# Layer 1 of a two-layer graph and expert network: the graph in blocks of 12, 8 and 6 row tiles, two early slot tables, and token lists dealt on GpSimd between gathers

## The chip, the cores and the metric

The kernel runs on one core of one Trainium2 chip, as one launch. The metric is device time in microseconds. A profile of one execution shows what each engine did: PE is TensorE (PEld its weight loads), DVE is VectorE, ACT is ScalarE, POOL is GpSimd, SP is SyncE, which here only issues transfers. L followed by a number is a line of the kernel before.

## The reference

The input is a matrix x of 3327 rows and 256 columns and an adjacency matrix of 3327 by 3327. Two layers follow each other, each a graph step and an expert step, both added to x.

```python
x = x + gnn0(layernorm(x), adj)          # mean over neighbours, then a linear map
x = x + ffn0(layernorm(x))               # 16 experts, top 2
h = layernorm(x)
Wh = h @ W
e = (Wh @ a[:256])[:, None] + (Wh @ a[256:])[None, :]
att = softmax(where(adj == 0, -1e9, e), axis=1)
x = x + leaky_relu(att @ Wh, 0.2)
f = layernorm(x)
p = softmax(relu(f @ router_w1 + b1) @ router_w2 + b2)      # 6 experts
w, i = top_k(p, 2); w = softmax(w)
out[e] = relu(relu(f @ w1[e] + c1[e]) @ w2[e] + c2[e]) @ w3[e] + c3[e]
x = x + sum of w * out[i]
```

The change concerns the last seven lines, layer 1.

## The kernel before

Rows stand in 26 tiles of 128, the last with 127 rows. Four tiles make a chunk, so there are seven chunks, the last of two tiles.

**The graph step** (`graph`) works through blocks of chunks. `GRAPH` for layer 1 is chunks 0 to 2, then 3 and 4, then 5, then 6: blocks of 12, 8, 4 and 2 tiles. For a block it walks through groups of source rows: `load_adj` brings a piece of the transposed adjacency matrix (L708, on SP), `mask_of` turns it into a 0/1 mask on DVE (L719), and PE multiplies the weighted rows y by it (L840) into PSUM. A mask holds at most 1536 columns, so a group is one source tile in the first two blocks, three in the block of four tiles and six in that of two. Three adj and three mask buffers are kept.

When a block's products are done, ACT and DVE copy the sums out (aT, L853 and L854), and a `finish` generator is made for each of its chunks. A generator's steps are: the final product with w1x and the update of x (L783), centring and normalising (L263 to L275), the store of the rows to the DRAM tensor hd (L794), transposes (L800), the router (L1268, `choose` L868) and `dispatch`. The steps of one block are called between the groups of the next block, two generators in turn (`in_turn`). Those of the last block run after the graph.

**dispatch** picks two experts per row on DVE, counts rows by expert with a small product (L356 to L360), and writes one entry per row and choice into the DRAM tensor list, by an indirect transfer from POOL (L387), two of them for each row tile: 52 in layer 1. An entry holds the place of the result, the row and the weight. The running counts are in seen1.

**The expert step** works in slots of 256 entries of one expert. There are 29 in the usual case, and more in a branch. `slot_table` turns the counts into a table: expert and place of each slot. The first table (`routed1`) is made after the first block's rows are counted and holds EARLY1 = 7 full slots; the second, the final one, is made after all rows are counted. A slot needs: `places`, which loads its 256 entries (who, L608, SP); `rows_in`, two indirect gathers from hd (xg, L616, POOL); `turned`, the transposes (L633); `layer1` twice (L1299); `out1` (L1311), with bias and weight on DVE (L1314, L1316); and `rows_out`, two indirect scatters to zd (L641, POOL). `slots1` runs these as a pipeline: in iteration s, out1 of slot s - 1, the second layer of s, the first layer of s + 1, the transposes of s + 2, the gathers of s + 3. There are three xg buffers. Expert weights of slots 0 to 6 come by one transfer each (v from w1d, 898 KB, L601). Those of later slots are copied on DVE (L1333) out of w_all, all six experts' weights, which are loaded after the graph (L1327), in memory that the graph's pools had.

In the program's text the slots stand after the graph:

```python
    graph("1", GRAPH, prepare1, 0.0, OP.not_equal, wx[1], update1, after1, 8, {(2, 0): routed1}, pools=pools1, ahead=ahead1, ready=list(REST))
    graph1.close()
    ...
    slots1(0, USUAL1)
```

A scheduler orders each engine's instructions, within `issue_after` marks. It keeps reads and writes of one DRAM tensor in order: a who load waits for the list writes that stand before it in the program, and a list write for the who loads before it. Layer 0 already deals the lists of its last blocks one by one: they are put into the list `due` and called from the loop of its slots.

Of the kernel before, what the change touches and what calls it, by code (L numbers as in the profile page):

```python
# [25 lines left out]
def kernel(  # L26
# [37 lines left out]
    GRAPH = [CHUNKS[:3]]  # L64
    while sum(map(len, GRAPH)) < len(CHUNKS):
        c = sum(map(len, GRAPH))
        GRAPH.append(CHUNKS[c : c + (2 if len(CHUNKS) - c > 2 else 1)])
# [15 lines left out]

    NE = sum(map(len, GRAPH[0]))
    assert NE <= NF
    EARLY1 = -(-(2 * NE * P - E1 * (S1 - 1)) // S1)

    USUAL1 = min(SLOTS1, int(2 * N / S1 + E1 / 2 + (E1 / 12) ** 0.5))
    LATE1 = USUAL1 - E1
    LOW = CHUNKS[: 4 * len(CHUNKS) // 7]  # L90
    assert EARLY1 < LATE1 and len(LOW) >= len(GRAPH[0])

# [3 lines left out]
    GRAPH0 = [CHUNKS[:3], CHUNKS[3:4], CHUNKS[4:]]  # L96
    NE0 = sum(map(len, CHUNKS[:4]))
    assert NE0 <= NF and len(GRAPH0[2]) <= 3
# [26 lines left out]
    hd_of = dram_disjoint_views(hd[:, :], 2)  # L125
# [176 lines left out]
    def dispatch(blk, logits, E, rows_of, seen, second_softmax):  # L302
# [15 lines left out]
        where = wheres[second_softmax]  # L318
        m, s, p = col("t_m"), col("t_s"), full("t_p")
# [63 lines left out]
        issued = []  # L383

        def listed(j, i):
            with in_turn_on_pool() if not second_softmax else nullcontext():
                ins = nc.gpsimd.indirect_dma_start(  # L387
                    out=rows_of[2 * (t0 + j) + i],
                    out_offset=bass.IndirectOffsetOnAxis(ap=idx[:, i, j : j + 1], axis=0),
                    in_=where[:, t0 + j, i, :], in_offset=None, bounds_check=E * NP - 1, oob_is_err=False,  # L390
                )
            if not second_softmax and blk in GRAPH0[2]:
                last["pool"] = ins
            if len(issued) > 1 and second_softmax and blk is GRAPH[1][-1]:
                tc.add_manual_dep(ins.ins, issued[-2], mybir.DependencyInfo(mybir.DependencyClass.Sync, mybir.DependencyReason.DATA))
            issued.append(ins.ins.name)

        for j in range(n):
            for i in range(2):
                if not second_softmax and blk in GRAPH0[2]:  # L400
                    due.append(lambda j=j, i=i: listed(j, i))
                else:
                    listed(j, i)
# [76 lines left out]
    def slot_table(E, seen, size, slot_p, first=None, taken=None, low=None, late=None, finals=False):  # L480
# [13 lines left out]
        def small(name, w=E, dtype=F32):  # L494
            return work.tile([P, w], dtype, name=name + ("e" if first else ""), bufs=1)
# [97 lines left out]
    def expert(table, s, E):  # L593

        with in_order():
            return (nc.sync.value_load(table[s : s + 1, 0:1], min_val=0, max_val=E - 1),
                    nc.sync.value_load(table[s : s + 1, 2:3], min_val=0, max_val=1))

    def load(tile_, source, which):
        e, new = which  # L600
        last["who"] = nc.sync.dma_start(tile_, source(bass.ds(e, 1)), cond=new, bounds_check="skip_entire_dma")  # L601

# [8 lines left out]
    def rows_in(who, of):  # L611

        n = who.shape[1]
        xg = io.tile([P, n, D], F32, name="xg", bufs=5 if n == 1 else 3)
        for h in range(n):
            last["pool"] = nc.gpsimd.indirect_dma_start(  # L616
                out=xg[:, h, :], out_offset=None, in_=of,
                in_offset=bass.IndirectOffsetOnAxis(ap=who[:, h, 1:2], axis=0),
            )
        return xg  # L620
# [17 lines left out]
    def rows_out(s, who, y):  # L638
        n = who.shape[1]
        for h in range(n):  # L640
            last["z"] = nc.gpsimd.indirect_dma_start(  # L641
                out=zviews[n * s + h], out_offset=bass.IndirectOffsetOnAxis(ap=who[:, h, 0:1], axis=0),
                in_=y[:, h, :], in_offset=None, bounds_check=2 * NP - 1, oob_is_err=False,
            )
            if s < LATE1:
                z_ready.append(last["z"].ins.name)
# [35 lines left out]
    def of_chunk(views, blk, ne):  # L682
        return views[0 if blk[-1] < ne else 1]
# [17 lines left out]
    def load_adj(adjs, block, g):  # L701

        c0, c1, cols, ce = columns(block)
        kr = rows(g[0])
        a = group_tile(adjs, I32, "adj", g, ce)
        src = adj_t[g[0] * P : g[0] * P + kr * len(g), c0:c1]
        if kr == P:
            last["adj"] = nc.sync.dma_start(a[:, :, :cols], src.rearrange("(t p) i -> p t i", p=P))  # L708
        else:
            for lo, hi in last_rows():  # L710
                nc.sync.dma_start(a[lo:hi, 0, :cols], src[lo:hi, :])
        return a
# [28 lines left out]

    def in_turn(those):

        now = []
        while those or now:
            while those and len(now) < 2:
                now.append(those.pop(0))
            for one in list(now):
                try:
                    next(one)  # L750
                    yield
                except StopIteration:
                    now.remove(one)
# [3 lines left out]
    def graph_pools(name, st):  # L757
        y = st.enter_context(tc.tile_pool(name=f"y{name}", bufs=1, side="right")).tile([P, NT, 2, D], F32R, name=f"y{name}")
        return y, *(st.enter_context(tc.tile_pool(name=f"{n}{name}", bufs=b, side="right"))
                    for n, b in (("adjs", AHEAD), ("big", AHEAD), ("tmp", 4)))  # L760
# [6 lines left out]
    def graph(name, blocks, prepare, value, op, wx, update, after, steps, routed, between=None, pools=None, ahead=(), ready=None, over={}, finish_with=None):  # L767
        adj_ahead, masks_ahead = ahead or ({}, {})
        with ExitStack() as st:
            y, adjs, big, tmp = pools or graph_pools(name, st)  # L770

            def finish(blk, aT):
# [4 lines left out]
                for i, t in enumerate(blk):  # L777
# [10 lines left out]
                    if i == 1 or i == n - 1:  # L788
                        centered(blk[i // 2 * 2 : i + 1], mv)
                        yield  # L790
                h = norm_centered(blk, mv)
                if name == "0":
                    store(blk)
                nc.scalar.dma_start(of_chunk(hd_of, blk, NE0 if name == "0" else NE)[t0 * P : (t0 + n) * P, :].rearrange("(t p) d -> p t d", p=P), h[:, :n, :])  # L794
# [489 lines left out]
    def routed1():  # L1284
        early["table"], early["had"] = slot_table(E1, seen1, S1, slot_p1, first=EARLY1)
        for s in range(EARLY1):
            who[s] = places(early["table"], s, E1, lists[1], S1)
# [4 lines left out]
    def layer1(s, i, src):  # L1292

        ps = bank(2 if s < EARLY1 or i == 0 else 1, [P, NC1, S1])
# [11 lines left out]
    def out1(s, who, h2):  # L1306
        ps = bank(1 if s < EARLY1 else 0, [P, 2, D])
# [9 lines left out]
        rows_out(s, who, y)  # L1317

    who = {}
    graph("1", GRAPH, prepare1, 0.0, OP.not_equal, wx[1], update1, after1, 8, {(2, 0): routed1}, pools=pools1, ahead=ahead1, ready=list(REST))  # L1320
    graph1.close()

    held = ctx.enter_context(tc.tile_pool(name="held", bufs=1, side="right"))
    w1_all = held.tile([P, E1, BB + 2 * 2], F32, name="w1_all")
    for e in range(E1):
        with in_order():
            last["who"] = nc.sync.dma_start(w1_all[:, e, :], w1d[e])  # L1327

    def weights_of(s):

        with tc.issue_after(last["dve"].ins) if "dve" in last else nullcontext():
            e = nc.vector.value_load(table1_of(s)[0][s - EARLY1 : s - EARLY1 + 1, 0:1], min_val=0, max_val=E1 - 1)
        last["copy"] = nc.vector.tensor_copy(w1s[s % 3], w1_all[:, bass.ds(e, 1), :].rearrange("p o w -> p (o w)"))  # L1333

    table1 = slot_table(E1, seen1, S1, slot_p1, taken=early["had"], low=seen_low, late=LATE1 - EARLY1, finals=True)

    def table1_of(s):
        return (early["table"], s) if s < EARLY1 else (table1, s - EARLY1)

    xg, xT, h1, h2, zs = {}, {}, {}, {}, {}  # L1340

    def slots1(first, end):
        for s in range(first - 3, end + 1):
            if first <= s - 1 < end:
                out1(s - 1, who[s - 1], h2.pop(s - 1))
            if first <= s + 2 < end:
                if s + 2 < EARLY1:
                    load(w1s[(s + 2) % 3], lambda e: w1d[e].rearrange("o p w -> p (o w)"), expert(*table1_of(s + 2), E1))
                else:
                    weights_of(s + 2)  # L1350
            known = EARLY1 if s < EARLY1 - 2 else end
            for i in range(max(who, default=-1) + 1, min(s + 5, known)):
                who[i] = places(*table1_of(i), E1, lists[1], S1)
            for i in range(max(xg, default=-1) + 1, min(s + 4, known)):
                xg[i] = rows_in(who[i], hd_of[0][: NE * P, :] if i < EARLY1 else hd[:, :])
# [4 lines left out]
            if first <= s + 2 < end:  # L1360
                xT[s + 2] = turned(xg[s + 2], 1 if s + 2 < EARLY1 else -1)
# [4 lines left out]
            if not first and s == LATE1 - 4:  # L1366
                or_any(table1, early["bad"])
            if not first and s == LATE1 - 2:
                with in_order():
                    early["low"] = nc.sync.value_load(table1_of(USUAL1)[0][USUAL1 - EARLY1 : USUAL1 - EARLY1 + 1, 4:5], min_val=0, max_val=1)  # L1370
# [5 lines left out]
            for i in SUMMED.get(s - LATE1, ()) if not first else ():  # L1376
                with tc.issue_after(last["copy"].ins), tc.issue_after(last["dve"].ins):
                    summed(LOW[i], zs[i])
                stored(nc.sync, LOW[i], zs.pop(i))

    LOADED, SUMMED = {1: (0, 1), 2: (2, 3)}, {2: (0,), 3: (1,), 4: (2, 3)}
    assert len(LOW) == 4 and max(SUMMED) < E1
    tail = ctx.enter_context(tc.tile_pool(name="tail", bufs=len(CHUNKS)))
    slots1(0, USUAL1)

    with more(*early["more"]):
        slots1(USUAL1, SLOTS1)
# [45 lines left out]
```

## Time and profile before

| | |
|---|---|
| runs, median of 3 | 1059.12 us (1056.38 to 1060.92) |
| profiled execution, its own time | 1021.54 us |
| its span, first to last instruction | 1018.8 us |
| granted TensorE clock, mean | 0.961 |
| PE, DVE, ACT, POOL busy | 934.6, 479.3, 282.6, 431.2 us |
| moved by DMA | 207.01 MB, 203 GB/s on average |
| graph of layer 1, last product | at 790.06 us |
| last slot's product | ends at 997.55 us |

The profiled execution is 37.6 us shorter than the median of the runs. The page gives busy time by engine, slices of the span, the chain that ended last and the costliest groups. Questions to the trace add stretches, timelines, and the time from a transfer's issue to its landing. Idle time is put down to the releaser that came last.

### The profile page before, as it was taken

Reading aid. Unit: us, or ns where it says so; the run is one execution under the profiler, and the core shown is the slowest. Engines: PE = TensorE matmul, PEld = TensorE weight load, DVE = VectorE, ACT = ScalarE, POOL = GpSimd, SP = SyncE. Lnnn points to the kernel's source line nnn. Section 1 sums busy time; section 2 is a strip of 40 time slices with the busy share of each in tenths; the row PEclk is TensorE's granted clock in tenths of the full one; section 3 lists DMA queues with packets and bytes.
Section 4 is the critical chain, followed back from the end, with each engine's and each line's share of the span. In section 5 each row is a group of like instructions: output and inputs, shape, how many; then the busy total and the mean of one; then the engine's idle time right before and its main releaser. Section 6 shows DMA issues by size and latency. Waiting matters only on the chain. (4 is left out here: it accounts for less than half of the span.)

```text
span 1018.8 us, 14334 instructions
## 1 busy us (share of the span) xinstructions
PE 934.6 (92%) x4505; PEld 781.8 (77%) x4505; DVE 479.3 (47%) x1747; ACT 282.6 (28%) x634; POOL 431.2 (42%) x407
## 2 busy tenths in 40 slices
PE   6999999889989799999999999999899579999991
PEld 5777878779878699888988787877678367888880
DVE  6565575245424122221212587557556442443773
ACT  3311330044311111111111443242142323344440
POOL 2040062522575445454544321004342375777771
PEclk9999999999998899999999999999899689999996
DMA  9988678855685566577888398868954965332376
GB/s 330 331 288 305 227 186 256 239 168 176 192 197 140 153 177 139 170 199 206 234 244 275 65 326 280 253 215 182 263 109 153 292 146 170 95 94 94 94 254 210
DMA packets 109329, 207.01 MB, mean 203 GB/s; under 512 B 30595, under 2 KB 63044, under 8 KB 109246
## 3 DMA queue, kind: packets, MB, share of 16 engines
q1 hardware_dynamic: 68384, 157.30, 49.5%
q0 software_dynamic: 20528, 30.56, 13.2%
q10 hardware_dynamic: 20334, 18.17, 5.6%
q8 instruction: 36, 0.59, 0.3%
q14 instruction: 47, 0.39, 0.1%
HBM read 176.82 MB, written 35.47 MB: 208 GB/s over the span
## 5 line engine op out<-in xcount | busy, mean ns | idle before, releaser
L840 PE MATMUL acc<-big,y 128*128 128x512 f32 (+2 forms) x1456 | 344.5, 390 | 27.1 <-DVE big L719 11.2
L840 PEld LDWEIGHTS acc<-big,y 128*128 128x128 f32 (+1 forms) x1456 | 263.6, 193 | 85.8 <-ACT y L896 7.5
L1074 PE MATMUL acc<-xT,w 128*128 128x256 f32 (+3 forms) x1024 | 214.4, 363 | 0.0
L1074 PEld LDWEIGHTS acc<-xT,w 128*128 128x128 f32 x1024 | 186.3, 200 | 17.0 <-issue 3.5
L387 POOL DMA_INDIRECT list<-where,t_idx x104 | 109.4, 1052 | 181.7 <-DVE t_idx L382 97.0
L719 DVE TENSOR_SCALAR big<-adj 128x1536 fp32r<-128x1536 int32 (+6 forms) x130 | 110.9, 857 | 115.4 <-DMA adj<-in_adj_t 82.9
L1097 PE MATMUL acc<-w,hid 128*128 128x256 f32 (+3 forms) x512 | 118.0, 381 | 0.0
L1082 DVE TENSOR_TENSOR hid<-hid,acc 128x512 f32<-128x512 f32 (+3 forms) x64 | 40.0, 624 | 151.4 <-PE acc L1074 144.3
L1104 POOL DMA_INDIRECT xd<-y,who x44 | 68.6, 1558 | 100.5 <-DVE y L1102 56.5
L1097 PEld LDWEIGHTS acc<-w,hid 128*128 128x128 f32 (+3 forms) x512 | 88.9, 177 | 20.3 <-issue 3.6
L1078 ACT ACTIVATE hid<-acc 128x512 f32<-128x512 f32 (+3 forms) x64 | 35.0, 547 | 205.3 <-PE acc L1074 193.8
L1302 ACT ACTIVATE h<-acc,v 128x256 f32<-128x256 f32 x116 | 55.0, 475 | 104.1 <-PE acc L1299 102.4
L616 POOL DMA_INDIRECT xg<-hd,who x58 | 66.9, 1154 | 29.5 <-issue 12.5
L641 POOL DMA_INDIRECT zd<-y,who x58 | 62.2, 1073 | 27.3 <-DVE y L1316 11.5
L1299 PE MATMUL acc<-xT,v 128*128 128x256 f32 x232 | 63.6, 398 | 6.2 <-DMA v<-w1d 5.6
L1299 PE MATMUL acc<-h,v 128*128 128x256 f32 x232 | 61.6, 389 | 0.6 <-ACT h L1302 0.6
L291 POOL TENSOR_TENSOR ln_var<-ln_var,half 128x2 f32<-128x2 f32 (+2 forms) x19 | 15.9, 837 | 101.4 <-DVE ln_var L289 88.3
L1104 POOL DMA_INDIRECT xd<-y,whos x20 | 31.7, 1586 | 62.0 <-DVE y L1102 47.1
L1314 DVE TENSOR_TENSOR y<-acc,v 128x512 f32<-128x512 f32 x29 | 20.0, 691 | 80.3 <-PE acc L1311 80.3
L1311 PE MATMUL acc<-v,h 128*128 128x256 f32 x232 | 56.9, 388 | 0.1
L1299 PEld LDWEIGHTS acc<-xT,v 128*128 128x128 f32 x232 | 44.6, 203 | 15.5 <-issue 5.2
L1049 POOL DMA_INDIRECT xg<-hd,who x44 | 43.0, 977 | 20.1 <-issue 11.6
(290 smaller groups left out, 982.5 us busy)
## 6 DMA issues: line engine op xcount, KB each, us to landing
adj<-in_adj_t SPq DMA_DIRECT2D x66, 768.0 KB, 6.6
w<-in_ffn_w SPq DMA_DIRECT2D x78, 512.0 KB, 5.7
adj<-in_adj_t SPq DMA_DIRECT2D x25, 639.5 KB, 6.4
adj<-in_adj_t SPq DMA_DIRECT2D x25, 512.0 KB, 4.4
v<-w1d SPq DMA_DIRECT2D x7, 898.0 KB, 7.1
hd<-ln_h ACTq DMA_DIRECT2D x12, 512.0 KB, 7.6
w_all<-w1d SPq DMA_DIRECT2D x6, 898.0 KB, 16.3
w1d<-in_ffn_w ACTq DMA_DIRECT2D x18, 256.0 KB, 4.3
```

The costliest lines, as they stand in the source:

```text
L387: ins = nc.gpsimd.indirect_dma_start(out=rows_of[2 * (t0 + j) + i], out_offset=bass.IndirectOffsetOnAxis(ap=idx[:, i, j : j + 1], axis=0), ...
L616: last["pool"] = nc.gpsimd.indirect_dma_start(out=xg[:, h, :], out_offset=None, in_=of, in_offset=bass.IndirectOffsetOnAxis(ap=who[:, h, 1 ...
L641: last["z"] = nc.gpsimd.indirect_dma_start(out=zviews[n * s + h], out_offset=bass.IndirectOffsetOnAxis(ap=who[:, h, 0:1], axis=0), in_=y[: ...
L719: last["mask"] = nc.vector.tensor_scalar(mask[:kr, :, :cols], a[:kr, :, :cols], value, None, op0=op)
L840: last["graph"] = nc.tensor.matmul(acc[c][k][:, :w], y[:kr, j, part, k * P : (k + 1) * P], mask[:kr, jj, i0 : i0 + w], start=(j == 0 and p ...
L1049: last["pool"] = nc.gpsimd.indirect_dma_start(out=xg[:m, h, :], out_offset=None, in_=hd_of[0][: NE0 * P, :] if s < AHEAD_E else hd[:, :], ...
L1074: last["slot"] = nc.tensor.matmul(q[:, c, :n], w[:, k, h0 : h0 + 2 * P - 1 : 2], xT[:, k, :n], start=(k == 0), stop=(k == KD - 1))
L1097: nc.tensor.matmul(ps[:m, h, :], hid[c // 2][:, c % 2, h * P : h * P + m], w3[:, c // 2, c % 2, :], start=(c == 0), stop=(c == NC0 - 1))
L1104: ins = last["pool"] = nc.gpsimd.indirect_dma_start(out=xd_of[2 + h] if s < USUAL0 else xd, out_offset=bass.IndirectOffsetOnAxis(ap=who[s] ...
L1299: ins = nc.tensor.matmul(ps[:, c, :], w[:, k, c : H1 : NC1], src[:, k, :], start=(k == 0), stop=(k == 1))
L1302: last["act"] = nc.scalar.activation(dst[:, c, :], ps[:, c, :], AF.Relu, bias=w1s[s % 3][:, BB + 2 * i + c : BB + 2 * i + c + 1])
L1311: nc.tensor.matmul(ps[:, h, :], h2[:, c, h * P : (h + 1) * P], w[:, c, :], start=(c == 0), stop=(c == NC1 - 1))
```

## The change

It does the following, in layer 1 alone.

1. The last two blocks of the graph become one, of 6 tiles (chunks 5 and 6). A group of it is two source tiles of 767 columns. The steps of block 0 are spread over 24 groups of block 1, those of block 1 over 12 of the 14 groups of block 2.
2. There are two early tables: 7 slots from chunks 0 to 2, 8 more from chunks 3 and 4. hd has three views, so that gathers of these slots wait for those chunks' stores alone. 14 slots are left for the final table.
3. The last block's finish steps are called from the loop of the slots (`beside1`, with the numbers of steps in `STEPS1`). The first three slots' weights, who loads and gathers follow the last adj load; w_all is loaded when the graph's pools are closed; weights from slot 3 on are copied from it.
4. List writes of chunks 3 to 6 (28) go into `due` and are called in the slots' loop by `DEALT1`. Every POOL transfer stands in a fixed turn (`in_turn_on_pool`), and a slot's scatters are held back by one slot.

```diff
-    GRAPH = [CHUNKS[:3]]
-    while sum(map(len, GRAPH)) < len(CHUNKS):
-        c = sum(map(len, GRAPH))
-        GRAPH.append(CHUNKS[c : c + (2 if len(CHUNKS) - c > 2 else 1)])
+    GRAPH = [CHUNKS[:3], CHUNKS[3:5], CHUNKS[5:]]
...
+    NE = [sum(map(len, CHUNKS[:c])) for c in (3, 5)]
+    EARLY1 = [-(-(2 * n * P - E1 * (S1 - 1)) // S1) for n in NE]
...
+    KNOWN1 = [n - 4 for n in EARLY1]
...
-    hd_of = dram_disjoint_views(hd[:, :], 2)
+    hd_of = dram_disjoint_views(hd[:, :], 3)
...
+        late = blk in (GRAPH[1] + GRAPH[2] if second_softmax else GRAPH0[2])
...
         def listed(j, i):
-            with in_turn_on_pool() if not second_softmax else nullcontext():
+            with in_turn_on_pool():
...
-                if not second_softmax and blk in GRAPH0[2]:
+                if late:
                     due.append(lambda j=j, i=i: listed(j, i))
...
+    def routed1(i):
+        n = EARLY1[i] - (EARLY1[i - 1] if i else 0)
+        table, had = slot_table(E1, seen1, S1, slot_p1, "ef"[i], first=n, taken=early.get("had"))
+        if i:
+            nc.vector.tensor_tensor(had, had, early["had"], op=OP.add)
+        tables1.append(table)
+        early["had"] = had
+
+    def started1(i):
+        with tc.issue_after(last["adj"].ins), in_order():
+            e = nc.sync.value_load(tables1[0][i : i + 1, 0:1], min_val=0, max_val=E1 - 1)
+        last["who"] = nc.sync.dma_start(w1s[i], w1d[bass.ds(e, 1)].rearrange("o p w -> p (o w)"))
+        who[i] = places(tables1[0], i, E1, lists[1], S1)
...
-            known = EARLY1 if s < EARLY1 - 2 else end
+            known = EARLY1[0] if s < KNOWN1[0] else EARLY1[1] if s < KNOWN1[1] else end
...
+            while len(outs) > (1 if not first and 2 <= s < LATE1 - 3 else 0):
+                outs.pop(0)()
+            yield
...
+    slots = slots1(0, USUAL1)
+    STEPS1 = {(-1, 1): 2, (0, 1): 2, (1, 1): 2, (2, 0): 2, (2, 1): 2, (3, 1): 2, (4, 0): 2}
+    DEALT1 = {-3: 2, -2: 2, -1: 2, 0: 4, 1: 3, 2: 3, 5: 2, 6: 2, 7: 2, 8: 2, 9: 2, 10: 2}
+
+    def beside1(post):
+        for i in range(3):
+            started1(i)
+        for i in range(3):
+            xg[i] = gathered1(i)
+        graph1.close()
+        early["w_all"] = held.enter_context(tc.tile_pool(name="held", bufs=1, side="right")).tile([P, E1, BB + 2 * 2], F32, name="w1_all")
+        for e in range(E1):
+            with in_order():
+                last["who"] = nc.sync.dma_start(early["w_all"][:, e, :], w1d[e])
+        next(post)
+        next(post)
+        xT[0] = turned(xg[0], -1)
+        for k, _ in enumerate(slots, 2 * -3):
+            s, half = divmod(k, 2)
+            for _ in range(STEPS1.get((s, half), 0)):
+                next(post, None)
+            if half:
+                for _ in range(DEALT1.get(s, 0)):
+                    due.pop(0)()
+                if s == 0:
+                    routed1(1)
+                if s == KNOWN1[1] - 1:
+                    break
...
+    graph("1", GRAPH, prepare1, 0.0, OP.not_equal, wx[1], update1, after1, 8, {(2, 0): lambda: routed1(0)},
+          pools=pools1, ahead=ahead1, ready=list(REST), over={1: 24, 2: 12}, finish_with=beside1,
+          tmp=tmp1.enter_context(tc.tile_pool(name="tmp1", bufs=4)))
...
+    tables1.append(slot_table(E1, seen1, S1, slot_p1, "", taken=early["had"], low=seen_low, late=LATE1 - EARLY1[1], finals=True))
+    for _ in slots:
+        pass
```

## The prediction

> **What bounds the kernel now.** I read the page first: PE is busy 92% of the span, POOL 42%, so TensorE's work sets the time except where the slices of PE dip. The largest dip past 600 us is at the end of the second graph, so I asked for busy time by stretches. The columns are length, then PE, PEld, DVE, ACT and POOL busy with instruction counts, the granted clock, the DMA share and GB/s.
>
> ```profile
> 780.00:790.00 10.00, 9.77 (x70) 9.16 (x68) 6.95 (x42) 3.50 (x12) 6.90 (x8) 1.00 0.03 3
> 790.00:800.00 10.00, 6.84 (x33) 4.08 (x32) 2.60 (x15) 5.36 (x11) 3.87 (x4) 0.97 0.86 231
> 800.00:810.00 10.00, 2.94 (x10) 1.48 (x8) 7.11 (x50) 1.95 (x7) 2.90 (x3) 0.50 1.01 319
> 810.00:820.00 10.00, 6.90 (x18) 4.37 (x19) 3.38 (x22) 2.90 (x7) 6.25 (x8) 0.50 1.01 369
> 820.00:830.00 10.00, 10.00 (x44) 7.99 (x43) 6.69 (x50) 3.47 (x8) 7.64 (x8) 0.84 0.16 45
> 830.00:840.00 10.00, 5.20 (x27) 4.33 (x26) 2.14 (x6) 2.47 (x5) 7.79 (x8) 1.00 0.87 146
> 880.00:900.00 20.00, 20.00 (x101) 17.54 (x100) 9.37 (x16) 8.96 (x19) 15.76 (x14) 1.00 0.31 93
> ```
>
> The graph's last product is at 790.06. From there to 840 PE is idle for 18 us and works at half clock for most of 800 to 823. From 880 on it is full. Next I read the timeline of PE, POOL and SP for what a slot costs and what holds the hole open (start, length, engine, line, operation, idle time before it and its releaser).
>
> ```profile
> 810.89 1.18 PE L800 MATMUL mm<-ident,ln_h 128*128 128x128 f32 x4 [5.43 <-ACT ln_h L275]
> 816.84 2.07 PE L1299 MATMUL acc<-xT,v 128*128 128x256 f32 x4 [0.83 <-DMA v<-w1d]
> 839.88 1.62 PE L1299 MATMUL acc<-xT,v 128*128 128x256 f32 x4 [4.80 <-DMA v<-w1d]
> 980.08 1.89 PE L1311 MATMUL acc<-v,h 128*128 128x256 f32 x8
> 985.75 1.89 PE L1311 MATMUL acc<-v,h 128*128 128x256 f32 x8
> 790.30 3.79 SPq L1327 DMA_DIRECT2D w_all<-w1d  x6
> 795.75 34.93 SPq L601 DMA_DIRECT2D v<-w1d  x4
> 883.26 0.97 POOL L616 DMA_INDIRECT xg<-hd,who  x1 [0.30 <-issue]
> 884.53 1.02 POOL L641 DMA_INDIRECT zd<-y,who  x1 [0.31 <-issue]
> ```
>
> A slot is 985.75 - 980.08 = 5.67 us of PE with nothing between. Gathers and lists follow each other on POOL every 1.27 us, scatters every 1.31, so a slot's two and two are 5.16 us there. The first slot starts only at 816.84, behind the last six tiles' finish (their chain of DVE, ACT and PE steps, one after the other) and behind a weight load issued at 795.75. The last PE work ends at 997.55; of the 207.5 us since 790.06, 29 x 5.67 = 164.4 are slots and 8 are the finish, so some 35 us are lost. Two landings matter below: the six loads of w_all, and lists in 820 to 826.
>
> ```profile
> DMA to landing us min/median/max: 12.6/16.3/20.5
> DMA to landing us min/median/max: 3.8/4.6/7.0
> ```
>
> **What the Trainium skill says.** "DMA: Bandwidth & Descriptors", section "Queues, rings and completion order": SP's transfers share one ring per DMA engine and descriptors are consumed in ring order. The trace agrees: the load of v issued at 795.75 behind w_all released PE only at 816.84, 21 us later, while one with nothing ahead (853.1) took 5.0. "TensorE: Matmul & The Clock Gate", section on the HAM clock gate: an idle array drops to half clock and returns after about 3.4 us of sustained work. The trace shows 0.50 from 800 on and full clock some 6.5 us after 816.84. Neither page is used for a price.
>
> **The change, part by part.** T is the end of the graph's last product.
>
> *Last block of 6 tiles.* The products are the same 728. From 728.79 to 790.06 the old blocks of 4 and 2 take 61.3 us. Out of this go: 16 matmuls of L783 for the 4-tile chunk, now after T (16 x 0.217 = 3.5); the wait of 0.85 at the dropped block border (773.58, aT); the wait of 1.00 at 763.76 for a mask whose adj load stood behind seven who loads on SP (750.58 to 757.9), which now come after all adj loads. T = 728.8 + 61.3 - 5.3 = 784.8, say 781 to 788. Mask elements and adj bytes are equal; I take DVE and the adj loads as covered as before.
>
> *PE work after T.* Finish of six tiles: L783 24 x 0.217 = 5.2, L800 12 x 0.12 = 1.4, L1268 2.6, L868 1.3, counts 0.9: 11.4. With 29 slots, 175.8 us. These are now interleaved in PE's order, so the chain of the finish hides behind slots 0 to 4. PE alone would end at 784.8 + 175.8 = 960.6, 37 us earlier. That is not reached, for POOL and SP.
>
> *Lists moved on POOL.* 28 list scatters (16 of chunks 3 and 4, 12 of 5 and 6), formerly at 781 to 834 with PE in its hole, now stand between gathers. In the built program's order list batches B and who loads alternate: every batch waits for the who load ahead of it (it reads the same list), and that who load waits until the batch before has landed. Behind the waiting list stand all gathers and scatters; PE waits for the gathers.
>
> *SP.* Three loads of v and three who follow the last adj load (in the old trace issued 15 us ahead of the graph's end): 2.7 MB at about 0.3 MB/us land by about T. w_all (5.4 MB) still waits for the graph's end, since it takes the graph's memory; four v loads (3.6 MB) are gone. At 319 to 369 GB/s it lands near T + 18. who 3 stands behind it in the ring: T + 19 (bounds T + 15, if it isn't held, as its own lists land about T + 12; and T + 24, if v runs past T or with the old 20.5). The fifth list, and so gather 3, wait for it.
>
> *POOL from there.* From list 5 to the second gather of slot 14 the order holds 24 lists, 24 gathers and 18 scatters: 48 x 1.27 + 18 x 1.31 = 84.6 us. Stalls: the loop list start, landing, who load, next batch. Lists land in 2.5 (780 to 789) to 4.6; I take 4.0, who loads 2.1 (what they take from 860 on), 0.1 for the wake: 6.2 us. Where a gather and a scatter stand between batches the cover is 1.28 + 2.54 + 2.62 = 6.4, no stall; at two batches with a gather alone it is 3.8: 2 x 2.4 = 4.8. A gather lands 3.2 us after its start. So slot 14's rows are there at T + 19 + 84.6 + 4.8 - 1.3 + 3.2 = T + 110.3. PE has by then 11.4 + 12 x 5.67 + 6.1 = 85.6 us of work ahead of its transposes, so it has waited some 25 us, spread over slots 3 to 14 (2 us each at the end, as 7.7 us of POOL stand against 5.67 of PE). From slot 15 POOL's 5.16 is below PE's 5.67 again: 175.8 - 85.6 = 90.2 us more. End of PE: 784.8 + 110.3 + 90.2 = 985.3, against 997.55: **12.2 us less**. Half clock after these waits is inside POOL's time.
>
> *DVE.* Four more weight copies (4 x 1.13) and one more slot table (some 30 x 0.17) make 10 us; DVE is busy 9.4 of 20 us beside the slots. The first copy waits for w_all to T + 18, with y of slot 1 and the logits behind it, which PE reaches near T + 24: nothing, at most 3 us if w_all is late. Deferred scatters wait for y that is a slot old: nothing.
>
> *Views, in_turn, finish's extra step, the tmp pool:* no instruction on an engine; bound -1 to +1 us. The stretch from the last matmul to the end (21.3 us) stays.
>
> Sum: the profiled execution's own time 1021.5 - 12.2 = 1009.3. The runs' median is 1059.12, 37.6 above it, which nothing in the trace explains; I carry it over unchanged: 1047. A slower PE in those runs would hide more of POOL's lists (up to 8 us more gain).
>
> **Rivals.** (1) *The list and who loop becomes the bound, and the kernel is slower.* For: lists in 820 to 826 landed after up to 7.0 us with the DMA nearly idle. With a loop of x us the stalls are 2(x - 3.8) + 8(x - 6.4), the second term above 6.4 only. At x = 7.6 the gain is gone; at 9.1 (7.0 + 2.1) the stalls are 32.2, 27.4 more: 1074. Against: 2.5 to 4.6 are usual. (2) *who 3 isn't held by w_all:* list 5 at T + 15, 4 us more: 1043. With the loop at 4.6 as well no stall but 1.6 is left: 1040. Against: the 21 us of v. (3) *v and w_all come later,* list 5 at T + 24, T itself 3 later: 1055, no difference to be told. (4) *The slots don't start under the finish,* for a missing weight or row: then 1059. Against: the order has slot 0 on PE ahead of the last ln_h transposes.
>
> **How the numbers follow.** Forecast 0.50 (1047, own range 1040 to 1053), rival 1 0.22 (1058 to 1075), rival 2 0.13 (1035 to 1043), rivals 3 and 4 0.15 (1053 to 1062). What can be told from no change is 0.5%, 5.3 us. Faster: 0.50 + 0.13 + 0.02 = 0.65; same: rivals 3 and 4 with the near edge of rival 1, 0.14; slower 0.21. The range 1034 to 1068 leaves out the far half of rival 1 and the best of rival 2.
>
> **What would show it.** Right: the graph's end near 785; slot matmuls within 10 us of it; POOL back to back for 85 us, PE's idle time there put down to xg; list batches released by who loads; w_all landing near T + 18 and list 5 with it; 7.7 us a slot for slots 10 to 14, then 5.67. Wrong: POOL idle for several us before each batch (rival 1), or lists 1 to 28 with no wait and PE full from T (more gain than forecast), or a graph that ends later than 788.

## The result, and the profile after

| | before | after |
|---|---|---|
| median of four runs each | 1060.02 us | 1071.30 us (1069.02 to 1074.31) |
| ratio, 95% interval | | 1.0105 (1.0056 to 1.0155) |
| forecast | | 1047 (1034 to 1068) |
| profiled execution, own time | 1021.54 | 1070.10 |

The change costs 11 us where a gain of 12 was forecast. The two profiled executions can't be subtracted from each other: that of before is 38 us below its timed runs, that of after is as long as its own. The experiments below bring profiles that can.

Stretches of the profile after follow, to be laid beside those shown of before. The graph's last product ends at 808.7 here (length, then PE, PEld, DVE, ACT and POOL busy with counts, granted clock, DMA share, GB/s).

```profile
808.70:818.70 10.00, 7.67 (x35) 6.16 (x36) 5.24 (x22) 5.31 (x17) 6.13 (x6) 1.00 0.89 345
818.70:828.70 10.00, 9.01 (x45) 7.65 (x44) 8.16 (x67) 7.47 (x19) 0.76 (x1) 1.00 0.72 238
838.70:858.70 20.00, 14.40 (x63) 11.68 (x62) 10.16 (x60) 4.91 (x13) 14.19 (x14) 0.83 0.19 41
858.70:878.70 20.00, 12.28 (x51) 9.17 (x51) 4.29 (x21) 3.07 (x6) 15.43 (x16) 0.86 0.31 81
```

The old hole is gone: in the first 20 us PE is busy 16.7, where before it was busy 9.8 of 790 to 810. A new, shallower one stands 30 to 70 us after the end: PE is busy 12 to 14 us of 20 there, at a mean clock of 0.83 and 0.86. POOL did one instruction between 818.7 and 828.7. The timelines of POOL and SP say why (start, length, engine, line, operation, idle time before it and its releaser).

```profile
808.76 3.15 SPq L1397 DMA_DIRECT2D w_all<-w1d  x6
815.69 1.24 POOL L384 DMA_INDIRECT list<-where,t_idx  x1 [0.30 <-issue]
827.94 1.07 POOL L384 DMA_INDIRECT list<-where,t_idx  x1 [11.01 <-DMA who<-list]
837.59 1.01 POOL L384 DMA_INDIRECT list<-where,t_idx  x1 [4.13 <-DMA who<-list]
```

POOL does four list writes, then nothing for 11 us until who 3 has landed. List 5 (the fifth list write after the graph) starts at the end + 19.2, and the same comes again with a wait of 4 us. The place and the releaser are those that the forecast named. Whether they are the cause, and what makes up the rest, was tested.

### The profile page after: what moved, and what is told of

It reads as the page before. It is cut to its first block, busy times and chain, and to the rows that moved or that the text cites. A ratio compares the mean times of both kernels' runs of the same rounds, so it can differ in the third digit from the quotient of the medians.

```text
span 1068.2 us, 14339 instructions
## 1 busy us (share of the span) xinstructions
PE 945.6 (89%) x4506; PEld 788.7 (74%) x4506; DVE 482.6 (45%) x1785; ACT 281.0 (26%) x634; POOL 430.2 (40%) x407
## 5 line engine op out<-in xcount | busy, mean ns | idle before, releaser
L705 DVE TENSOR_SCALAR big<-adj 128x1536 fp32r<-128x1536 int32 (+5 forms) x128 | 111.2, 873 | 107.6 <-DMA adj<-in_adj_t 44.3
L601 POOL DMA_INDIRECT xg<-hd,who x58 | 59.3, 1022 | 63.8 <-PE acc L831 36.9
L1303 PE MATMUL acc<-h,v 128*128 128x256 f32 x232 | 64.4, 399 | 23.0 <-ACT h L1306 20.5
L627 POOL DMA_INDIRECT zd<-y,who x58 | 68.3, 1178 | 34.4 <-DVE y L1320 19.7
L1303 PEld LDWEIGHTS acc<-h,v 128*128 128x128 f32 x232 | 45.2, 204 | 33.1 <-ACT h L1306 23.8
L1315 PE MATMUL acc<-v,h 128*128 128x256 f32 x232 | 59.4, 399 | 2.3 <-ACT h L1306 1.6
L289 POOL TENSOR_TENSOR ln_var<-ln_var,half 128x2 f32<-128x2 f32 (+2 forms) x19 | 15.3, 804 | 102.8 <-DVE ln_var L287 79.1
```

The lines of the kernel that those rows point to most:

```text
L601: last["pool"] = nc.gpsimd.indirect_dma_start(out=xg[:, h, :], out_offset=None, in_=of, in_offset=bass.IndirectOffsetOnAxis(ap=who[:, h, 1 ...
L627: last["pool"] = nc.gpsimd.indirect_dma_start(out=zviews[n * s + h], out_offset=bass.IndirectOffsetOnAxis(ap=who[:, h, 0:1], axis=0), in_= ...
L705: last["mask"] = nc.vector.tensor_scalar(mask[:kr, :, :cols], a[:kr, :, :cols], value, None, op0=op)
L1303: ins = nc.tensor.matmul(ps[:, c, :], w[:, k, c : H1 : NC1], src[:, k, :], start=(k == 0), stop=(k == 1))
L1315: nc.tensor.matmul(ps[:, h, :], h2[:, c, h * P : (h + 1) * P], w[:, c, :], start=(c == 0), stop=(c == NC1 - 1))
```

## The experiments

Ratios are to the kernel before, run beside each on the same chip. That kernel took 1010 to 1013 us beside most experiments and 1051 to 1060 beside a few, the result above among them; I call these the quick and the slow sets. Where nothing is said, it was a quick one. The record numbers the chips of the quick sets 3, 4, 5 and 9, and those of two slow ones 5 and 14, so it doesn't show that the chip makes the difference. "End" is the end of the graph's last product in that profile, and "gather 14" the second of slot 14's two gathers. A "loop" is the turn of list batch, who load and next list batch.

### The same two kernels again

No edit; each of them was run twice more beside the other, and before once more by itself.

> The kernel before, unchanged, for a second profile. Theory A (the profiled execution of before was not a usual one; usual ones hold stretches in which every hand-over between PE, ACT and DVE takes 3 to 4 us longer, as the profile after shows at 140 to 158 us in code of layer 0 that the change does not touch): its own time is 1055 to 1065, graph 1 starts near 590 instead of 575, and the missing 38 us are found in such stretches. Rival B (that profile is usual and only the timed runs are longer): its own time is 1018 to 1030 again. Ratio 1.000.

> The changed kernel, unchanged, beside before on the same chip. If the 1.0105 of the first runs is the change's: ratio 1.006 to 1.015 again. If it came from the chip or from chance: 0.995 to 1.005. The stall of 11.64 us at 959 us of its first profile: theory A (it wanders) puts it elsewhere or nowhere this time; rival B (it belongs to a slot, behind the release of a y buffer by a late scatter) puts it at slot 14 again.

> The changed kernel beside before on the same chip: ratio 1.008 to 1.016 on either kind of chip, if the list and who loop and POOL's bound are the cause; list 5 at the graph's end + 19 to + 22 and slot 14's second gather at + 118 to + 124.

> The kernel before, for a profile from this chip. On the quick chip: own time 1002 to 1025, no idle time put down to an unknown releaser. On a slow one: own time 1045 to 1065, and PE, ACT and DVE idle for 30 us or more in hand-overs of 3 to 8 us, in layer 0 too, which the change does not touch.

> The kernel before, for a profile. If it falls on a slow chip (own time 1045 to 1065): idle time of PE, ACT and DVE put down to an unknown releaser, 30 us or more in sum, in layer 0 and 1 alike, and graph 1 starts near 590. On the quick chip (1002 to 1025): none.

Before_again: 1.0001 (0.9976 to 1.0027), own time 1002.64. After_again: 1.0120 (1.0083 to 1.0158), own time 1027.26. After_third: 1.0135 (1.0085 to 1.0185). Before_third: 1.0016 (0.9990 to 1.0042). Before_fourth: 0.9989 (0.9959 to 1.0020), in a slow set. So the loss is the change's, in quick and slow sets alike. The profiles of the first four show no idle time with an unknown releaser, and their stretches can be compared. First after_again, cut at graph 1's first product, at the end, at list 5, at gather 14 and at PE's last product:

```profile
574.30:776.70 202.40, 197.03 (x935) 158.09 (x936) 132.15 (x568) 66.23 (x172) 41.97 (x41) 0.99 0.80 240
776.70:797.20 20.50, 18.18 (x91) 15.24 (x90) 13.86 (x90) 13.24 (x36) 4.90 (x6) 1.00 0.94 312
797.20:898.90 101.70, 82.25 (x346) 65.97 (x345) 38.47 (x146) 31.41 (x67) 70.68 (x65) 0.88 0.27 55
898.90:1004.20 105.30, 97.68 (x445) 83.52 (x445) 54.97 (x77) 38.16 (x77) 76.31 (x67) 0.94 0.46 139
```

Then before_again, cut at graph 1's first product, at the end and at PE's last product:

```profile
564.38:777.14 212.76, 202.93 (x954) 160.55 (x955) 137.16 (x588) 69.63 (x183) 50.40 (x50) 0.99 0.74 217
777.14:979.04 201.90, 184.96 (x862) 154.24 (x860) 97.81 (x254) 80.54 (x168) 139.05 (x128) 0.93 0.51 160
```

The graph is 10 us shorter and the slots are 26 longer. The second pair of profiles has 213.0 and 206.1 for before, 202.3 and 222.6 for after. The means of the two are 212.9 and 204.0 against 202.3 and 225.0: -10.6 and +21.0, together +10.4, near the 11 to 14 us by which the timed runs differ. When graph 1 starts varies by itself: from 564.4 to 577.7 in the profiles of the quick sets, in code that no experiment touches, so whole spans of single executions don't tell 10 us.

Before_fourth fell into a slow set, with an own time of 1052.81. Some of the waits of its engines, and then of those in the profile after, also from a slow set, are these (us in total, times, longest):

```profile
DVE hid L1082 <- remote: 17.2, 3, 6.5
ACT xT L635 <- remote: 11.1, 2, 8.6
```

```profile
DVE y L1318 <- remote: 30.4, 2, 17.6
DVE hid L1073 <- remote: 14.4, 2, 7.9
```

"Remote" means that no releaser is found in the trace. Such waits of several us stand in both kernels there, in both layers (81 us in sum in before_fourth, 127 in the profile after), and in no profile from a quick set. The profile of before that the forecast was made from has none: it looks like an execution of the quick kind, beside timed runs of the slow kind. After's wait of 11.64 us is in neither later profile, so it belongs to no slot there. Theory A named the right stretches, but its numbers fell with B's, since 1002.64 us is neither: the profile of 1021 us was unusual only for the runs that it was shown with.

### The merged block alone

```diff
-    while sum(map(len, GRAPH)) < len(CHUNKS):
-        ...
+    GRAPH += [CHUNKS[3:5], CHUNKS[5:]]
```

This is the kernel before with that and nothing else.

> The kernel before with the graph's blocks of 12, 8 and 6 tiles and nothing else of the change. The step of the forecast that takes 5.3 us off the graph: from graph 1's first product to its last 205 to 209 us (212.8 in the second profile of before). After it all six tiles' finish stands in the hole, with 12 lists more, so the first slot starts 5 to 12 us later after the graph's end than the 27.1 of before. Sum 0 to +8 us, ratio 1.000 to 1.008. Rival (merging is free only with the interleaving): the graph stays at 211 to 214 and the ratio is 1.008 to 1.015.

Both ranges of the ratio were missed, on the good side: 0.9966 (0.9939 to 0.9994), 3.4 us less than before. The graph took 206.8 us (575.22 to 781.97), as expected, and the first slot's layer began at the end + 25.1, no later than the 27.1 of before_again. So the block of 6 tiles is a small gain by itself, also without the interleaving; the expected 5 to 12 us in the hole did not come.

### who loads and list batches

```diff
 def beside1(post):
     for i in range(3):
         started1(i)
+    for i in range(3, EARLY1[0]):                 # who_first
+        who[i] = places(tables1[0], i, E1, lists[1], S1)
```

```diff
-            for i in range(max(who, default=-1) + 1, min(s + 5, known)):        # who_second
+            for i in range(max(who, default=-1) + 1, min(s + (5 if first or s != KNOWN1[0] else EARLY1[1]), known)):
```

Who_first has the first edit, who_second the second, who_all both. POOL's order and its instructions stay as in after; only what they wait for changes.

> The changed kernel with the who loads of slots 3 to 6 issued together with those of slots 0 to 2, ahead of the six loads of w_all and, in program order, of the first list batch. Theory C: list 5 no longer waits for who 3 behind w_all, so it starts near the graph's end + 8 instead of + 19; gathers 3 to 6 are some 10 us earlier and the time is 5 to 12 us below after. Rival D: PE is not waiting for these rows for more than 3 to 5 us, within 4 us of after. Rival F: weights of slot 3 wait for w_all until the graph's end + 18 in any case, so at most 3 us are won.

> The changed kernel with only the second half of that edit: who loads of slots 7 to 14 together, those of slots 3 to 6 as in after, behind w_all. If the two waits add up: some 8 us less than after, ratio 1.000 to 1.006. If the wait of list 5 for who 3 behind w_all is alone what counts: ratio 1.009 to 1.016, as after.

> As who_first, and the who loads of slots 7 to 14 issued together as soon as the 16 lists of chunks 3 and 4 are dealt, ahead of the last 12 lists; the POOL order is that of after, so only waits go. Theory C1 (the alternation of list batch and who load is what POOL loses; in who_first it still idles 2.1 to 2.8 us before each of the six late batches and gathers 8 to 14 come every 8.2 to 10.2 us): gathers 8 to 14 every 7.7 us, slot 14's second gather near the graph's end + 84 instead of + 93, and 5 to 12 us less than who_first, ratio 0.982 to 0.989. Rival C2 (POOL's own 7.7 us a slot is the whole loss once who 3 is mended): ratio 0.990 to 0.997, as who_first.

> who_all once more, beside the next one. If its gain is the same wherever it runs: 0.982 to 0.993. If on a slower chip hand-overs between PE, ACT and DVE hide or eat it: 0.993 to 1.010, with PE waits of 5 us and more for ACT's h.

| kernel | ratio | list 5 | gather 14 | PE's last product |
|---|---|---|---|---|
| after_again | 1.0120 (1.0083 to 1.0158) | end + 20.5 | + 122.2 | + 227.5 |
| who_second | 1.0059 (1.0027 to 1.0090) | + 19.2 | + 113.3 | + 218.4 |
| who_first | 0.9939 (0.9914 to 0.9963) | + 8.0 | + 102.9 | + 207.6 |
| who_all | 0.9871 (0.9816 to 0.9926) | + 8.0 | + 98.6 | + 203.9 |

Theory C held in both halves, and the halves add up: by ratio 18 us and 6 us, 25 together. The first half gave more than the 5 to 12 us expected of it, and gather 14 of who_all came later than the + 84 expected, since its gathers 8 to 14 stand 8.2 us apart and not 7.7. Who_all_again came to 0.9892 (0.9848 to 0.9937), again in a quick set. With every other instruction of the change in its place and only the order of who loads mended, the change gains 11 to 13 us there instead of losing 12 to 14. Rival D (less than 4 us) and expectation F (weights of slot 3 hold it up anyway) fell. The loop that is broken by the second edit looks like this in after_again:

```profile
875.84 0.97 POOL L384 DMA_INDIRECT list<-where,t_idx  x1 [0.30 <-issue]
882.14 0.37 SPq L592 DMA_DIRECT2D who<-list  x1
885.41 0.97 POOL L384 DMA_INDIRECT list<-where,t_idx  x1 [2.50 <-DMA who<-list]
```

From the batch's last list to the issue of the next who it takes 6.3 us, from there to the next batch 3.3: 9.6 together, and POOL has work for 7.4 of them. In who_all, at the same batches, POOL goes on:

```profile
871.61 0.97 POOL L384 DMA_INDIRECT list<-where,t_idx  x1 [0.30 <-issue]
872.88 0.97 POOL L384 DMA_INDIRECT list<-where,t_idx  x1 [0.30 <-issue]
874.15 1.73 POOL L601 DMA_INDIRECT xg<-hd,who  x1 [0.30 <-PE acc L1303]
```

Is it w_all's transfers that make the first loop so long? W_all_late issues them behind who 3:

```diff
-        for e in range(E1):
-            ... early["w_all"][:, e, :] ...       # before the slots
+            if k == -2:                           # after who 3
+                ... the same six loads
```

> The changed kernel with the six loads of w_all issued behind who 3 instead of ahead of it; the order of who loads and list batches stays. Theory G (the transfers of w_all make the first loop of list batch, who 3 and list 5 long): batch 1 lands some 5 us after its start, who 3 is issued near the graph's end + 9, list 5 starts near + 12 instead of + 20, and w_all lands near + 26, just before slot 3's layers need its weights: 5 to 9 us less than after, ratio 1.002 to 1.008. Rival H (the loop of batch and who load is as long without them): list 5 at + 18 to + 21, and slot 3 waits for its weights, so 0 to 6 us more than after, 1.010 to 1.018.

Both theories had half of it. The ratio is 1.0131 (1.0027 to 1.0235), as H says, though four runs give an interval too wide to shut out G's range. List 5 moved as G says. POOL's timeline (end at 782.8):

```profile
795.07 0.97 POOL L384 DMA_INDIRECT list<-where,t_idx  x1 [4.64 <-DMA who<-list]
814.31 1.01 POOL L384 DMA_INDIRECT list<-where,t_idx  x1 [14.44 <-DMA who<-list]
```

List 5 starts at the end + 12.2 after a wait of 4.6, and now the next loop, behind who 4, waits 14.4. From the end to PE's last product it is 227.7 us, no less than in after. In both places that were tried for w_all, the long wait fell on the loop that ran while its 5.4 MB were on their way; in who_first, which has no loop there, list 5 doesn't wait.

### Lists earlier

```diff
-        late = blk in (GRAPH[1] + GRAPH[2] if second_softmax else GRAPH0[2])
+        late = blk in (GRAPH[2] if second_softmax else GRAPH0[2])
```

Lists_early has this on after. Lists_before_end has it on who_all, with `over={1: 24, 2: 8}`.

> The changed kernel with the 16 list writes of chunks 3 and 4 issued as soon as they are made, during the graph's last block; the 12 of the last block are still dealt. Theory C (the lists between gathers hold the slots back): POOL has 16 x 1.27 = 20 us less between list 5 and slot 14's rows and 6 batches fewer wait for who loads; slot 14 starts at the graph's end + 90 instead of + 121, and the time is 10 to 25 us below after. Rival D (PE, ACT and DVE hand-overs set the slots' pace): within 5 us of after. Rival E (the lists stand on POOL ahead of the finish's own work in the graph and delay the masks): the graph ends 3 to 8 us later, gain below 10.

> who_all with the steps of block 1's finish spread over 8 groups of block 2 instead of 12, and the 16 lists of chunks 3 and 4 issued when they are made, so mostly before the graph's end, ahead of gathers 0 to 2; the 12 of the last block are dealt as before. If POOL's work after the graph's end is what is left of the loss: 16 x 1.27 = 20 us less of it there, slot 14's second gather near the end + 78 instead of + 97, ratio 0.975 to 0.984. If the lists come too late or the denser steps hold up the masks: first slot 5 to 15 us later or a graph 3 to 8 us longer, ratio 0.988 to 1.000.

Lists_early came to 1.0146 (1.0099 to 1.0194), no better than after, and lists_before_end to 1.0071 (1.0040 to 1.0102), 18 to 20 us more than who_all and worse than either expectation. The 16 lists run only from the end - 4 to the end + 16 in the first, and from the end - 7 to the end + 14 in the second. POOL and PE in lists_before_end (end at 783.0):

```profile
775.93 1.16 POOL L384 DMA_INDIRECT list<-where,t_idx  x1 [29.61 <-DVE t_at L361]
```

```profile
807.70 1.10 PE L618 MATMUL mm<-ident,xg 128*128 128x128 f32 x4 [20.35 <-DMA who<-list]
```

The lists wait for DVE's places of the rows, with denser steps too, and who 0 to 2 and their gathers now follow the lists, so the first layer of slot 0 starts at the end + 30 and + 26 instead of + 7. Rival D's range for lists_early (within 5 us of after) was met, but by this new wait and not for D's reason. Expectation E had the wrong place: the graph took 204.3 and 205.5 us, inside the 202.3 to 208.2 of the other quick profiles with these blocks and the interleaving. Dealing the lists behind the first gathers is worth more than the 20 us of POOL that it seems to cost.

### What bounds the last slots

Extra_gather is after with one more indirect transfer on POOL ahead of the gathers of slots 15 to 25.

```diff
 def gathered1(i):
+    if EARLY1[1] <= i < 26:
+        more_xg = io.tile([P, 3], I32, name="more_xg", bufs=1)
+        with in_turn_on_pool():
+            last["pool"] = nc.gpsimd.indirect_dma_start(out=more_xg, ..., in_=lists[1][:, :], ...)
```

> The changed kernel with one more indirect transfer on POOL (12 bytes per row, into a tile that nobody reads) ahead of the gathers of slots 15 to 25. Theory I (POOL, late at slot 14, stays the bound to the end, since its 5.2 to 5.7 us a slot leave nothing to catch up): all of 11 x 1.3 = 14 us are added, ratio 1.021 to 1.030. Rival J (from slot 15 on PE is the bound again, as the forecast has it, and the last 12 us come from its clock or from the loads of results): POOL has 11 x 0.5 us to spare, so 0 to 8 us, 1.010 to 1.019.

The ratio is 1.0262 (1.0159 to 1.0365), 13 to 14 us above after's two; the interval is wide, but the trace speaks for theory I as well. PE then waits for rows in each of the slots concerned, for example

```profile
920.43 0.51 PE L618 MATMUL mm<-ident,xg 128*128 128x128 f32 x2 [0.96 <-DMA xg<-hd,who]
927.18 0.51 PE L618 MATMUL mm<-ident,xg 128*128 128x128 f32 x2 [0.81 <-DMA xg<-hd,who]
```

a slot every 6.8 us. So POOL has nothing to spare there. It doesn't follow that POOL alone is the bound without the extra transfer: in after_again PE has one wait, of 0.56 us, between 908 and 980. The two are level.

The next runs leave POOL's sum of work unchanged and move other things: who_all_no_hold (`while outs:`) no longer holds scatters back, and who_all_late_results and late_results_again have `LOADED` and the sums one to two steps later.

> who_all with a slot's scatters not held back: each follows the gathers of the same step. If the hold does what its place says (POOL doesn't wait for y of the slot that PE is in): without it POOL waits for DVE's y in front of the scatters of the early slots, gathers come later, 3 to 8 us slower than who_all. If POOL is in any case behind PE: within 3 us, and the scatters of two slots that stand together where the hold ends (2.6 us of POOL) are gone.

> who_all with the four loads of results (z) of the early rows, 2 slots later than there, and their sums as late. Theory K (the last rows land late because these loads run at the same time: in after's second profile a gather issued beside them landed in 6.2 us, where 3.3 is usual, PE waited 3.1 and fell to half clock for part of 25 us): the last gathers land in 3 to 4 us, PE is full to the end, 3 to 6 us less than who_all, ratio 0.981 to 0.985, if the later sums don't stand at the end. Rival L (POOL's order, two slots' scatters ahead of one gather, makes these rows late): within 2 us. Rival M (the sums now stand behind the last slot): 2 to 8 us more.

> who_all with the loads of results two slots later, beside who_all on one chip. If the 1.0117 was the edit's: 20 to 28 us more than who_all. If it was the chip's: within 8 us of who_all (rival M, late sums behind the last slot, 2 to 8 us more; theory K, 3 to 6 us less).

Who_all_no_hold: 0.9897 (0.9868 to 0.9927), not to be told from who_all; the hold is worth nothing that can be measured here. Late_results_again: 0.9895 (0.9853 to 0.9937) beside 0.9892 of who_all_again. The time is rival L's, but the two traces show K and M at once. The stretch from gather 14 to PE's last product, first in late_results_again, then in who_all_again:

```profile
877.90:978.30 100.40, 93.82 (x451) 80.63 (x450) 50.22 (x75) 39.20 (x80) 76.29 (x67) 1.00 0.41 123
876.40:980.70 104.30, 95.43 (x447) 81.98 (x445) 53.24 (x77) 38.69 (x78) 76.14 (x67) 0.97 0.47 140
```

It is 4 us shorter at full clock, since the last gathers land in 2.8 to 3.6 us, not in up to 7.3, as K says. From there to the program's end it takes 25.0 us instead of 20.8, as M says. In these two executions the one eats the other.

Who_all_late_results ran in a slow set and came to 1.0117 (1.0075 to 1.0159) there. Since the edit makes no difference in a quick set, most of this is probably the set's, and then who_all's gain doesn't hold there. From the end to PE's last product before_fourth took 224.8 us, the first profile of after 238.6 and this kernel 232.8, with PE waits such as

```profile
854.71 2.08 PE L1303 MATMUL acc<-h,v 128*128 128x256 f32 x4 [7.06 <-ACT h L1306]
```

Who_all itself was not run in a slow set, and what makes hand-overs long there stays open. So the cause of the loss is tested in the quick sets, where after loses 1.2 to 1.4%. In the slow set of the result itself the profile shows the same two waits on POOL, but the one kernel without them that ran in a slow set, who_all_late_results, doesn't gain there.

## Why the prediction was wrong, point by point

All numbers are counted from the end, as in the forecast; "measured" is the mean of after_again and after_third, for before that of before_again and before_third.

| step | forecast | measured |
|---|---|---|
| graph, against before | -5.3 | -10.6 |
| list 5 starts | 19 | 19.9 |
| from there to gather 14 | 88.1 | 101.1 |
| from there to PE's last product | 93.4 | 104.0 |
| sum of the last three | 200.5 | 225.0 |
| the same in before | 207.5 | 204.0 |
| sum against before | -12.2 | +10.4 |

- **The last block of 6 tiles: right,** and by more than was taken: with it the graph took 202.3 to 208.2 us in the quick profiles, without it 212.8 to 215.1. Alone it gives 3.4 us.
- **The slots under the finish: right.** The first slot's layer starts at the end + 7 to 9 in both kinds of profile, and PE is busy 18.2 of the 20.5 us to list 5.
- **List 5 at T + 19: right** in time and cause. That the order was the cause and could be mended was not seen: the forecast booked it as fixed.
- **The step that failed first is "POOL from there", in its size.** It is 13.0 us longer than forecast. The mechanism is rival 1's, the alternation of list batch and who load. Two terms of it were mis-sized, by 6 to 7 us each. First the loop: I took 4.0 for the lists, 2.1 for the who load and 0.1 for the wake, 6.2 us, with 6.4 of cover. In after_again the last list of the late batches started 7.0 to 9.6 us before the next batch, 8.1 on average: 2.3 to 6.3 from the last list to the issue of who, and mostly 3.3 from there to the next list, not 2.2. A loop shorter than its cover gives nothing back, so its spread costs, not only its mean. Second POOL's own time: I took 1.27 and 1.31 us from two lines of a timeline. The groups of the profile before had the means all along (busy us and mean ns after the bar):

```profile
L616 POOL DMA_INDIRECT xg<-hd,who x58 | 66.9, 1154 | 29.5 <-issue 12.5 <-PE acc L1299 9.6 <-PE acc L840 7.1
L641 POOL DMA_INDIRECT zd<-y,who x58 | 62.2, 1073 | 27.3 <-DVE y L1316 11.5 <-issue 9.1 <-DVE y L1314 5.2
```

  With 0.30 between, that is 1.45 a gather, 1.37 a scatter and (1.05 by its group) 1.35 a list: 92 us for the 66 instructions where I summed 84.6. In the stretch of 101.7 shown above POOL is busy 70.7; with 0.30 at each of its 65 instructions 11.5 us are left as waits, against 4.8 in the forecast. Who_all has no such waits and takes 90.6 us for the same 65, where the forecast had 83.3.
- **The second step that failed is "From slot 15 POOL's 5.16 is below PE's 5.67 again: 90.2 us more",** by 10.6 us. With the means a slot's two and two are 5.65 on POOL, level with PE's 5.67. The profile before showed this in the same stretch, at the gather ahead of the one that I read:

```profile
881.50 1.45 POOL L616 DMA_INDIRECT xg<-hd,who  x1 [0.30 <-issue]
887.15 1.46 POOL L616 DMA_INDIRECT xg<-hd,who  x1 [0.30 <-issue]
```

  So POOL, too, started a slot every 5.65 us there, with nothing to spare. What the 10.6 us are (11.9 in after_again alone) is seen on PE in after_again: it waits for the rows of slot 14 and for those of the last gather, and runs at half clock after each of these waits.

```profile
901.94 1.10 PE L618 MATMUL acc<-ident,xg 128*128 128x128 f32 x4 [3.70 <-DMA xg<-hd,who]
983.58 0.70 PE L618 MATMUL mm<-ident,xg 128*128 128x128 f32 x2 [3.12 <-DMA xg<-hd,who]
```

```profile
901.94:906.00 4.06, 4.06 (x12) 3.40 (x13) 0.00 (x0) 0.58 (x1) 2.33 (x3) 0.50 0.32 71
920.00:940.00 20.00, 20.00 (x101) 17.62 (x100) 9.24 (x13) 9.44 (x19) 15.73 (x15) 1.00 0.28 89
984.00:988.00 4.00, 4.00 (x12) 3.19 (x11) 2.43 (x3) 0.58 (x1) 1.51 (x2) 0.50 1.06 393
```

  Once it has slot 14's rows PE takes 102.3 us to its last product, 12.1 above the 90.2. Its waits in them are 4.2 us (0.56, 3.12 and 0.56). Half clock in 8 us after each of the two long waits (0.50, then 0.82 and 0.83) costs 5.4 us, an estimate from these clocks; the rest is open. So "Half clock after these waits is inside POOL's time" failed at these two, and the last gather was taken to land in 3.2 us but landed in 6.2, beside four loads of results of 1 MB each (issued from 976.45). Late_results_again above has neither that wait nor that half clock. Who_all, without the loops, still needs 105.3 us in this stretch, and who_all_again 104.4.
- **w_all, DVE, views and the tail after the last product:** nothing else was found. The tail is 21 us in after and before alike, and DVE's added copies don't show.
- **The rivals.** Rival 1 had the mechanism and the sign, and the 1071 lies in its range, but in part by luck. Its formula gives 2 x (8.1 - 3.8) + 8 x (8.1 - 6.4) = 22 us of stalls for a loop of 8.1, twice the 11.5 that are there, since POOL's longer own time covers more of the loop (6.9 to 7.4 us at the late batches, not 6.4). I gave it 0.22, from "2.5 to 4.6 are usual", though the 7.0 stood beside them. Rival 2 fell (who 3 is held); of rival 3 w_all came in time; rival 4 fell.
- **The 37.6 us carried over** were right to carry: they go with the set, and after loses much the same in both, 1.05% in the slow one and 1.2 to 1.4% in the quick ones.
- **Who_all's 11 to 13 us less** are close to the 12.2 of the forecast, but that is chance: it also lacks the wait for list 5, which the forecast had booked, and this pays for what the forecast had too small.

## What to carry to other kernels

When loads and stores of one tensor take turns in the program, each turn is a round trip through two queues, 8.1 us on average here; issue all loads whose data is complete ahead of the next store batch, before trimming anything else. Price an engine that may become the bound by the mean of its groups, not by a clean line of a timeline, and ask whether it has anything to spare after the stretch in which it falls behind: here 14 us put on POOL far from the waits came out as 13 to 14 us of time. Add what a wait leaves behind it, here half clock on PE, also for the last wait. Compare a wait with its cover by its spread, since early arrivals don't pay for late ones.

## What the runs showed of the hardware

- With w_all's six loads on their way, a who load of 3 KB landed in 6.3 us in after_again and 6.7 in w_all_late; later in after_again it was 1.8 to 2.5. The loop around it, from last list to next list, took 15.3 and 18.0 us, where 8.1 is the mean of the late ones. The gathers beside four loads of 1 MB landed in up to 6.2 to 7.3 us, without them in 2.8 to 3.6.
- Indirect transfers on POOL take 0.97 us in most lines and 1.5 to 1.7 in every few: in the late slots of after_again 965, 976 and 1462 ns are the least, middle and longest of 13 gathers. What makes the long ones long is open.
- After waits of 3.70 and 3.12 us PE's granted clock was 0.50 for the next 4 us, 0.82 and 0.83 in the 4 after them, and then 1.00.
- One kernel took 1013 us in one set and 1053 in another, with the clock within 0.02 (0.973 and 0.954 in profiles). In the slow sets ACT and DVE wait up to 12.3 and 17.6 us with no releaser in the trace; in the quick ones not once. The record numbers the chip 5 in both, so whether it is the chip or its condition stays open.
